# One 256-column product for two layers: node 1's tile times the sending weights of layers 2 and 3 in a four-layer graph kernel

## The chip, the cores and the metric

The kernel runs on one core of one Trainium2 chip. The metric is the device time of one execution in microseconds (us). Three executions of the kernel before took 1271.45, 1272.61 and 1273.16 us, so its median is 1272.61 us.

A core has engines with queues of their own: TensorE (PE in the profile: matmuls, with the loading of their stationary operand listed apart as PEld), VectorE (DVE), ScalarE (ACT), GpSimd (POOL) and SyncE (SP, which here issues DMAs). Matmul results land in PSUM. This kernel treats PSUM as 8 banks, each 128 partitions by 512 fp32 numbers.

## What is computed

x is (32, 512, 128) and adj is (32, 512, 512), symmetric, of zeros and ones. For each of the 32 batches four graph layers follow one another, each as x = x + layer(relu(layernorm(x)), adj): a masked attention, a graph convolution whose weights come out of an LSTM, a block of four "sending and receiving" layers, and a last linear aggregation. The change is in the third, cut here to what matters:

```python
for i in range(4):
    # nodes of layer 0: h; of 1: n1; of 2: [n2, n1]; of 3: [n3, n1, h]
    src_agg = einsum('bjv,bij->biv', nodes @ ws + bs, l2norm(adj, 2))
    dst_agg = einsum('bjv,bji->biv', nodes @ wd + bd, l2norm(adj, 1))
    self_rep = nodes @ wn + bn
    nodes_next = tanh(concat([src_agg, self_rep, dst_agg]) @ wu + bu)
```

With a symmetric adj both aggregations are one. The kernel multiplies the weights together in advance, so that each layer needs one "sending" weight (128x128 per input chunk) and one "own" weight. The inputs by chunk are `CHUNKS = ([0], [1], [2, 1], [3, 1, 0])`: node 1 (the output of layer 0) is an input of layer 2 and again of layer 3.

## The kernel before

The work is cut by batch. A first pass goes over all batches, then an LSTM of 128 steps runs with a second pass over the batches beside it, and the rest, `rest(b, turn, ...)` at L1632, goes through the batches in 32 "turns", one batch each. The chains of several turns overlap.

The order of the instructions is written by a planner (`class Plan`), not by the program text. Each step is handed to it as an op with an engine, a cost in us, what it reads and what it writes (`PE(...)`, `ACT(...)`, `DVE(...)`). The planner takes the ops by rank, which for a turn k grows by 12 per turn and falls with the length of the chain behind the op, and lays them on the engines as they become ready; the result is a fixed order of each engine's queue. It also hands out the buffers. A tile asked for with `bank(...)` takes one of the 8 PSUM banks from the first op that uses it to the end of the last. A rule in `room` keeps the last free bank for ops that are at most 12 in rank behind the most urgent one. `LEAD` is a lift in rank for the last turn's steps that are marked with `R + 4`.

Within a turn, layer i of the third block (L1719 to L1741 in `rest`) has these steps:

- **Fill** (L1012 on ScalarE or L1016 on VectorE, whichever the planner finds earlier): the bias row is copied into a bank `f_py` of 4 x 128 columns, once the layer before has done its L1733.
- **Sending product** (L1726): for each of the four 128-row tiles of the batch, one fp32 matmul with 128 moving columns per input chunk, added on top of the bias. The stationary operand is the node's tile, the moving one the weight. Layers 0 to 3 have 4, 4, 8 and 12 of these. The order of the chunks in layer 3 is nodes 3, 1, 0.
- **Split** (`split`, L1509): ScalarE rounds the bank to fp32r (L1513), and VectorE takes the remainder (L1514), both of 512 columns.
- **Aggregation** (L1555): two times four matmuls of 512 columns, of the rounded part and of the remainder with the squared adjacency `f_ar`, into a bank `f_pa`.
- **Scale** (L1733, VectorE), **own product** (L1737: one fp32 matmul of 512 columns per chunk, into the same bank) and **tanh** (L1741, ScalarE), which makes the next node.

In the trace an fp32 matmul appears as two PE instructions ("passes") with a weight load each, so the 4 products of layer 0 are 8 records, the 12 of layer 3 are 24. An fp32r matmul, such as those of the aggregation, is one record. Some matmul records are missing from the trace. In the names of the profile `f_n` is a node 1, 2 or 3, and `f_T_c` (in a few turns `f_hT_c`) is node 0.

The last turn does its layer 3 in halves of 256 columns (`layer_by_halves`): its splits are L1590 and L1591, its own products are L1609, with 256 moving columns. After the layers a turn transposes node 4 and adds it to x, normalises, aggregates once more (`f_pg`), multiplies (`f_p`, L1791) and stores.

The weights of the sending and own products are in `wf`, 7 chunks by 2 kinds by 128 columns; `W_F = [0, 1, 2, 4]` is the first chunk of each layer, so that node 1's sending weights of layers 2 and 3 are chunks 3 and 5.

Of the kernel before, what the change touches and what calls it, by code (L numbers as in the profile page):

```python
# [13 lines left out]
P = 128  # L14
# [470 lines left out]
FR = mybir.dt.float32r  # L485
# [3 lines left out]
W_F = [0, 1, 2, 4]  # L489
# [304 lines left out]
def symmetric(ctx, tc, x, adj, weights, cols, rows, lstm_b, prelu_a, out, fail):  # L794
# [12 lines left out]
    nc = tc.nc  # L807
    B, N, D = x.shape
    NT = N // P
# [11 lines left out]
    Q_FIRST = range(0)  # L821
    RESIDENT = range(3)
    FIRST_GAPS = (2.0, 3.5, 4.0, 4.0)
    LEAD = 3.0
    Q_AT = 3
    MOVED = range(2, B - 2)
    BY_HALVES = (3,)
    HALVED = 1
    PUT_OFF = (B - 3, B - 2)
    WAITING = (B - 2,)  # L830
    TURN = 32
# [25 lines left out]
    def f32(ap):  # L857
        return ap.bitcast(FP)
# [145 lines left out]
    def fill(rank, dst, src, r, c, after, beside=False):  # L1004

        def mark():
            if not c.marked:
                nc.tensor.matmul(c.t, marks[:, :P], marks[:, : c.size], start=True, stop=True)

        def act():  # L1010
            mark()
            nc.scalar.copy(dst(), src)  # L1012

        def dve():
            mark()
            nc.vector.tensor_copy(dst(), src)  # L1016
        return plan.op({"ACT": (t_act(c.size), act), **({} if beside else {"DVE": (t_dve(c.size), dve)})}, rank, r, [c], after)

    def bias(k, n=NT):
        return brow[:, k, :].unsqueeze(1).to_broadcast([P, n, P])  # L1020
# [155 lines left out]
    def pass_1(b, pos):  # L1176
        R = 10_000 + pos * 10
        xc = new("x", (P, NT, P), f"f_x_{b}")
        n = 2 if pos < HALVED else NT
# [330 lines left out]
    def split(rank, src, name):  # L1510

        parts = new("y", (P, NT, 2, P), f"f_y_{name}", FR)
        ACT(rank, t_act(N), lambda: nc.scalar.copy(parts.t[:, :, 0, :], src.t), [src], [(parts, 0)])  # L1513
        DVE(rank, t_dve(N), lambda: nc.vector.tensor_sub(parts.t[:, :, 1, :], src.t, f32(parts.t[:, :, 0, :])),  # L1514
            [src, (parts, 0)], [(parts, 1)])
        return parts
# [34 lines left out]
    def aggregate(rank, parts, ar, pg):  # L1551

        def half(k):
            for j in range(NT):
                nc.tensor.matmul(pg.t, parts.t[:, j, k, :], ar.t[:, j, :], start=(k == 0 and j == 0),  # L1555
                                 stop=(k == 1 and j == NT - 1))

        def both():
            half(0)
            half(1)  # L1560
        if rank < plan_rest:
            last = PE(rank, 8 * t_r(N), both, [parts, ar], [pg], count=16)
            last.patience = PATIENCE
            return last
        for k in range(2):
            last = PE(rank, 4 * t_r(N), lambda k=k: half(k), [(parts, k), ar], [pg])
        return last

    def state_of(b, lw):
# [5 lines left out]
    def layer_by_halves(R, b, i, nodes, ar, inv_row, before):  # L1575

        nch = L2_CHUNKS[i]
        parts = new("y", (P, NT, 2, P), f"f_y_{b}_{i}", FR)
        for at in range(0, NT, HALF):
            part = slice(at, at + HALF)  # L1580
            py = bank(f"f_py_{b}_{i}_{at}", (P, HALF, P), whole=False, filled=True)
            fill(R, lambda py=py: py.t, bias(i, HALF), [(biases, i)], py, [before])

            def sent(py=py, at=at):
                for j in range(HALF):
                    for c, n in enumerate(CHUNKS[i]):
                        nc.tensor.matmul(py.t[:, j, :], nodes[n].t[:, bass.ts(at + j, P)], wf[:, W_F[i] + c, 0, :], start=False,
                                         stop=(c == nch - 1), skip_group_check=True)
            PE(R, HALF * nch * t_mm(P), sent, [nodes[n] for n in CHUNKS[i]], [py])
            ACT(R, t_act(HALF * P), lambda py=py, part=part: nc.scalar.copy(parts.t[:, part, 0, :], py.t), [py], [(parts, (0, at))])  # L1590
            DVE(R, t_dve(HALF * P), lambda py=py, part=part: nc.vector.tensor_sub(parts.t[:, part, 1, :], py.t, f32(parts.t[:, part, 0, :])),  # L1591
                [py, (parts, (0, at))], [(parts, (1, at))])
        n = new(f"n{i + 1}" if i < 3 else "gs", (P, N), f"f_n{i + 1}_{b}")
        nodes.append(n)
        for at in range(0, NT, HALF):
            cols = slice(at * P, (at + HALF) * P)
            pa = bank(f"f_pa_{b}_{i}_{at}", (P, HALF * P), whole=False)
            for k in range(2):
                for half in range(0, NT, HALF):
                    def quarter(pa=pa, cols=cols, k=k, half=half):  # L1600
                        for j in range(half, half + HALF):
                            nc.tensor.matmul(pa.t, parts.t[:, j, k, :], ar.t[:, j, cols], start=(k == 0 and j == 0),
                                             stop=(k == 1 and j == NT - 1))
                    PE(R, HALF * t_r(HALF * P), quarter, [(parts, (k, half)), ar], [pa], count=2 * HALF)
            before = DVE(R, t_dve(HALF * P), lambda pa=pa, cols=cols: nc.vector.tensor_mul(pa.t, pa.t, inv_row.t[:, cols]), [inv_row], [pa])

            def own(pa=pa, cols=cols):
                for c, m in enumerate(CHUNKS[i]):
                    nc.tensor.matmul(pa.t, wf[:, W_F[i] + c, 1, :], nodes[m].t[:, cols], start=False, stop=(c == nch - 1),  # L1609
                                     skip_group_check=True)  # L1610
# [21 lines left out]
    def rest(b, turn, lw_after):  # L1632
# [81 lines left out]
            n0, before = ln_t(R, xn, "n0", f"c{b}")  # L1714
        nodes = [n0]
        for i, nch in enumerate(L2_CHUNKS):
            if turn == B - 1 and i in BY_HALVES:
                before = layer_by_halves(R + 4, b, i, nodes, ar, inv_row, before)
                continue  # L1719
            py = bank(f"f_py_{b}_{i}", (P, NT, P), filled=True)  # L1720
            fill(R, lambda py=py: py.t, bias(i), [(biases, i)], py, [before])

            def sent(py=py, i=i, nch=nch):
                for j in range(NT):
                    for c, n in enumerate(CHUNKS[i]):
                        nc.tensor.matmul(py.t[:, j, :], nodes[n].t[:, bass.ts(j, P)], wf[:, W_F[i] + c, 0, :], start=False,  # L1726
                                         stop=(c == nch - 1), skip_group_check=True)
            PE(R, 4 * nch * t_mm(P) - 0.01, sent, [nodes[n] for n in CHUNKS[i]], [py])
            parts = split(R, py, f"{b}_{i}")
            pa = bank(f"f_pa_{b}_{i}")  # L1730

            aggregate(R, parts, ar, pa)
            before = DVE(R, t_dve(N), lambda pa=pa: nc.vector.tensor_mul(pa.t, pa.t, inv_row.t), [inv_row], [pa])  # L1733

            def own(pa=pa, i=i, nch=nch):
                for c, n in enumerate(CHUNKS[i]):
                    nc.tensor.matmul(pa.t, wf[:, W_F[i] + c, 1, :], nodes[n].t, start=False, stop=(c == nch - 1),  # L1737
                                     skip_group_check=True)
# [6 lines left out]
        two = turn == B - 1 and 3 in BY_HALVES  # L1745
        if two:
            end4 = update_by_halves(R, b, nodes[4], xc)
        elif moved:
# [194 lines left out]
```

## Time and profile before

| what | value |
|---|---|
| median of three executions | 1272.61 us |
| the profiled execution | 1272.32 us |
| its span, first to last instruction | 1270.4 us |
| PE busy | 1251.3 us, 98% of the span |
| PEld, DVE, ACT, POOL busy | 970.2, 974.8, 835.6, 389.6 us |
| DMA | 232.81 MB, 183 GB/s in the mean |
| granted TensorE clock | 0.999 |
| share of PE in the chain that ended last | 83% |

The page lists groups of instructions as "line engine operation, output<-inputs, shapes, count | busy us, mean ns of one | idle time before them". A mean of one matmul is longer than the distance to the next, since matmuls are pipelined. The distance is read from the chain of waits, which in the last stage runs along PE alone and lists its pieces with start and length.

### The profile page before, as it was taken

What the parts mean: (1) busy time and instruction counts of PE and PEld (TensorE: products, weight loads), DVE (VectorE), ACT (ScalarE), POOL (GpSimd) and SP (SyncE); (2) the same over time, 40 slices, a digit from 0 to 9 for tenths busy, and PEclk for the clock granted to TensorE, in tenths of its full rate; (3) what the DMA queues carried; (4) which work ended last, traced back from release to release, by engine and by line L of the source; (5) the groups of instructions that cost most, each with busy time, mean ns of one, the idle gap of its engine ahead of it and who ended that gap; (6) DMA issues with size and microseconds to landing.
All of it is one profiled execution on the core that took longest, in us unless ns stands there. A gap on an engine that the chain in (4) does not pass through costs nothing.

```text
span 1270.4 us, 33137 instructions
## 1 busy us (share of the span) xinstructions
PE 1251.3 (98%) x12078; PEld 970.2 (76%) x12078; DVE 974.8 (77%) x3267; ACT 835.6 (66%) x2126; POOL 389.6 (31%) x737
## 2 busy tenths in 40 slices
PE   9999999999999999999999999999999999999998
PEld 7988976766776767777778778778787787787776
DVE  7899979889888889775777677677667676787655
ACT  5666777777777766774566666666666666675434
POOL 4565542322322225332213213123123132232101
PEclk9999999999999999999999999999999999999999
DMA  8888887788678778769367677676676677743211
GB/s 291 257 265 275 277 275 225 220 266 254 211 239 283 229 208 211 144 174 219 76 146 176 153 166 164 152 178 152 155 177 154 154 173 158 170 88 96 50 25 45
DMA packets 313725, 232.81 MB, mean 183 GB/s; under 512 B 152145, under 2 KB 258386, under 8 KB 313554
## 3 DMA queue, kind: packets, MB, share of 16 engines
q1 hardware_dynamic: 296096, 213.50, 59.7%
q0 software_dynamic: 16896, 16.78, 8.4%
q8 instruction: 97, 1.59, 0.6%
q14 instruction: 74, 0.61, 0.2%
q10 hardware_dynamic: 562, 0.33, 0.1%
HBM read 136.25 MB, written 62.84 MB: 157 GB/s over the span
## 4 chain that ended last, share of the span: by engine, by line
PE 83%; DVE 7%; DMA 4%; ACT 3%; POOL 2%; issue 1%; SPq 0%; DVEq 0%; ACTq 0%
PE f_pa L1555 17%; PE f_py L1726 15%; PE f_pa L1737 15%; PE f_pg L1555 7%; PE f_s L1421 4%; PE f_po L1427 3%; PE f_z L1315 3%; PE f_pol L1263 2%; PE f_pk L1189 2%; PE f_p L1791 2%; PE f_sl L1253 2%; PE f_pv L1231 2%; PE f_pl L1688 2%; PE f_pd L1288 2%; DMA f_dx<-f_x 1%
## 5 line engine op out<-in xcount | busy, mean ns | idle before, releaser
L1555 PE MATMUL f_pa<-f_ar,f_y 128*128 128x512 f32 x1016 | 295.9, 429 | 0.2 <-DVE f_st_r L1093 0.2
L1555 PEld LDWEIGHTS f_pa<-f_ar,f_y 128*128 128x128 f32 x1016 | 187.9, 188 | 72.9 <-issue 38.3
L1726 PE MATMUL f_py<-f_wf,f_n 128*128 128x128 f32 x1264 | 171.7, 275 | 0.1
L1726 PEld LDWEIGHTS f_py<-f_wf,f_n 128*128 128x128 f32 x1264 | 162.5, 192 | 9.2 <-issue 1.4
L1737 PE MATMUL f_pa<-f_n,f_wf 128*128 128x512 f32 x316 | 150.6, 592 | 0.0
L1741 ACT ACTIVATE f_n<-f_pa,f_bcol 128x512 f32<-128x512 f32 x127 | 88.2, 694 | 92.6 <-PE f_pa L1737 92.6
L1468 ACT ACTIVATE f_ar<-f_a 128x512 fp32r<-128x512 f32 x228 | 141.2, 622 | 6.5 <-DMA f_a<-in_adj_dram 4.3
L1475 POOL DMA_DIRECT2D f_das<-f_ar x32 | 27.1, 845 | 361.2 <-ACT f_ar L1468 356.2
L1513 ACT CAST f_y<-f_py 128x512 fp32r<-128x512 f32 x127 | 74.8, 589 | 80.8 <-PE f_py L1726 78.5
L1514 DVE TENSOR_TENSOR f_y<-f_py,f_y 128x512 fp32r<-128x512 f32 x127 | 87.1, 687 | 48.9 <-ACT f_y L1513 46.2
L1427 PEld LDWEIGHTS f_po<-f_v,f_e 128*32 128x32 f32 x3072 | 91.6, 110 | 27.1 <-issue 20.4
L1427 PE MATMUL f_po<-f_v,f_e 128*32 128x129 f32 x3072 | 109.6, 273 | 1.1 <-DVE f_e L1425 0.7
L1733 DVE TENSOR_TENSOR f_pa<-f_pa,f_inv 128x512 f32<-128x512 f32 x127 | 86.0, 695 | 27.3 <-PE f_pa L1555 27.2
L1421 PE MATMUL f_s<-f_q,f_k 128*32 128x384 f32 x928 | 93.9, 486 | 0.4 <-issue 0.4
L1737 PEld LDWEIGHTS f_pa<-f_n,f_wf 128*128 128x128 f32 x316 | 57.7, 190 | 47.7 <-issue 43.7
L1315 PE MATMUL f_z<-f_w,f_seq 128*32 128x128 f32 x2040 | 83.2, 276 | 7.3 <-DVE f_seq L1361 5.0
L1315 PEld LDWEIGHTS f_z<-f_w,f_seq 128*32 128x32 f32 x2040 | 53.1, 109 | 47.3 <-issue 12.2
L1484 DVE SCALAR_TENSOR_TENSOR f_aT<-f_a,f_aT 128x1024 bf16<-128x1024 f32 (+1 forms) x68 | 76.1, 1153 | 1.2 <-DMA f_aT<-f_das 1.2
L1144 DVE COPY f_hl_d<-f_n 128x1024 uint16<-128x1024 uint16 x28 | 19.4, 694 | 73.7 <-ACT f_n L1741 73.6
L1726 PE MATMUL f_py<-f_wf,f_T_c 128*128 128x128 f32 x448 | 72.8, 275 | 0.1
L1555 PE MATMUL f_pg<-f_ar,f_xp_d 128*128 128x512 f32 x248 | 71.2, 410 | 0.0
L1424 ACT ACTIVATE f_e<-f_s 128x384 f32<-128x384 f32 x128 | 60.7, 484 | 13.1 <-PE f_pg L1555 7.7
(234 smaller groups left out, 2762.1 us busy)
## 6 DMA issues: line engine op xcount, KB each, us to landing
f_a<-in_adj_dram SPq DMA_DIRECT2D x116, 256.0 KB
f_a<-in_adj_dram SPq DMA_DIRECT2D x28, 1024.0 KB
f_das<-f_ar POOLq DMA_DIRECT2D x32, 512.0 KB, 4.7
f_dkq<-f_kh SPq DMA_DIRECT2D x29, 448.0 KB
f_al<-in_adj_dram SPq DMA_DIRECT2D x32, 256.0 KB
f_inv<-f_ddi SPq DMA_DIRECT2D x32, 256.0 KB
f_x<-in_x_dram SPq DMA_DIRECT2D x31, 256.0 KB
out_dram<-f_x SPq DMA_DIRECT2D x31, 256.0 KB
```

The source lines that it names most:

```text
L1315: nc.tensor.matmul(z.t[part, k, :, :], h, w[:, m : m + 4, part], start=False, stop=True, skip_group_check=True)
L1421: PE(R, t_mm(NR), lambda s=s, j=j: quarters(lambda p: nc.tensor.matmul(s.t[p], keys_of()[:, j * P + p.start : j * P + p.stop], q_of(), sta ...
L1427: PE(R, t_mm(P), lambda e=e, t=t, j=j: quarters(lambda p: nc.tensor.matmul(po.t[p, t, :], e.t[:, t * P + p.start : t * P + p.stop], v.t[:, ...
L1468: ACT(rank, 0.62, lambda t=t: nc.scalar.activation(ar.t[:, t, :], a.t[:, t, :], AF.Square, accum_out=deg.t[:, t : t + 1]), [(a, t)], [(ar, ...
L1484: nc.vector.scalar_tensor_tensor(flat(aT.t[:, n * k : n * (k + 1), :]), flat(a.t[:, n * k : n * (k + 1), :]), 1.0, flat(aT.t[:, n * k : n ...
L1513: ACT(rank, t_act(N), lambda: nc.scalar.copy(parts.t[:, :, 0, :], src.t), [src], [(parts, 0)])
L1514: DVE(rank, t_dve(N), lambda: nc.vector.tensor_sub(parts.t[:, :, 1, :], src.t, f32(parts.t[:, :, 0, :])), [src, (parts, 0)], [(parts, 1)])
L1555: nc.tensor.matmul(pg.t, parts.t[:, j, k, :], ar.t[:, j, :], start=(k == 0 and j == 0), stop=(k == 1 and j == NT - 1))
L1726: nc.tensor.matmul(py.t[:, j, :], nodes[n].t[:, bass.ts(j, P)], wf[:, W_F[i] + c, 0, :], start=False, stop=(c == nch - 1), skip_group_chec ...
L1733: before = DVE(R, t_dve(N), lambda pa=pa: nc.vector.tensor_mul(pa.t, pa.t, inv_row.t), [inv_row], [pa])
L1737: nc.tensor.matmul(pa.t, wf[:, W_F[i] + c, 1, :], nodes[n].t, start=False, stop=(c == nch - 1), skip_group_check=True)
L1741: ACT(R, 0.57, lambda pa=pa, n=n, i=i: nc.scalar.activation(n.t, pa.t, AF.Tanh, bias=bcol[:, i : i + 1]), [pa], [n])
```

## The change

In turns 2 to 27, layers 2 and 3 share two banks. Each bank holds two of the four row tiles, and for each tile 128 columns of layer 2 and 128 of layer 3. Both banks are filled with both bias rows before layer 2. In layer 2 each tile of node 1 is multiplied once with 256 columns, the weights of both layers side by side; node 2 follows with 128 columns for layer 2. In layer 3 only nodes 0 and 3 are left, with 128 columns each. The sending products of layer 2 are two PE ops now, one for each bank, and so are those of layer 3. Each layer's split is done bank by bank: two ScalarE copies and two VectorE subtractions of 256 columns instead of one of 512. Aggregation, scale, own product and tanh stay as they are. Besides, `LEAD` goes from 3.0 to 4.0. `HEAD_TILES = 2` and `HALF_TURNS = (B - 1,)` are names for values that were written out before, and `aggregate` now accepts parts with halves of their own.

```diff
-    LEAD = 3.0
+    LEAD = 4.0
...
+    SHARED = range(2, B - 4)
+    HEAD_TILES = 2
+    HALF_TURNS = (B - 1,)
...
-            last = PE(rank, 4 * t_r(N), lambda k=k: half(k), [(parts, k), ar], [pg])
+            last = PE(rank, 4 * t_r(N), lambda k=k: half(k), [(parts, q) for q in parts.parts if (q[0] if isinstance(q, tuple) else q) == k] + [ar], [pg])
...
-            py = bank(f"f_py_{b}_{i}", (P, NT, P), filled=True)
-            fill(R, lambda py=py: py.t, bias(i), [(biases, i)], py, [before])
...
-            PE(R, 4 * nch * t_mm(P) - 0.01, sent, [nodes[n] for n in CHUNKS[i]], [py])
-            parts = split(R, py, f"{b}_{i}")
+            if turn in SHARED and i > 1:
+                if i == 2:
+                    pys = [bank(f"f_py_{b}_2_{h}", (P, 2, 2, P), filled=True) for h in range(2)]
+                    for py in pys:
+                        fill(R, lambda py=py: py.t, brow[:, 2:4, :].unsqueeze(1).to_broadcast([P, 2, 2, P]), [(biases, 2), (biases, 3)], py, [before])
+                for h, py in enumerate(pys):
+                    def sent(py=py, i=i, h=h):
+                        for j in range(2):
+                            of = [bass.ts(2 * h + j, P)] * 3
+                            if i == 2:
+                                nc.tensor.matmul(py.t[:, j, :, :], nodes[1].t[:, of[0]], wf[:, W_F[2] + 1 : W_F[3] + 2 : 2, 0, :], start=False,
+                                                 stop=False, skip_group_check=True)
+                                nc.tensor.matmul(py.t[:, j, 0, :], nodes[2].t[:, of[0]], wf[:, W_F[2], 0, :], start=False, stop=True, skip_group_check=True)
+                            else:
+                                nc.tensor.matmul(py.t[:, j, 1, :], nodes[0].t[:, of[0]], wf[:, W_F[3] + 2, 0, :], start=False, stop=False, skip_group_check=True)
+                                nc.tensor.matmul(py.t[:, j, 1, :], nodes[3].t[:, of[0]], wf[:, W_F[3], 0, :], start=False, stop=True, skip_group_check=True)
+                    PE(R, 2 * (t_mm(2 * P) + t_mm(P)) if i == 2 else 4 * t_mm(P), sent, [nodes[n] for n in ((1, 2) if i == 2 else (0, 3))], [py])
+                parts = new("y", (P, NT, 2, P), f"f_y_{b}_{i}", FR)
+                for h, py in enumerate(pys):
+                    part = slice(2 * h, 2 * h + 2)
+                    ACT(R, t_act(2 * P), lambda py=py, part=part, i=i, parts=parts: nc.scalar.copy(parts.t[:, part, 0, :], py.t[:, :, i - 2, :]), [py], [(parts, (0, h))])
+                    DVE(R, t_dve(2 * P), lambda py=py, part=part, i=i, parts=parts: nc.vector.tensor_sub(
+                        parts.t[:, part, 1, :], py.t[:, :, i - 2, :], f32(parts.t[:, part, 0, :])), [py, (parts, (0, h))], [(parts, (1, h))])
...
```

More of the change, by code (lines that the diff above doesn't have):

```diff
@@ L1178, in pass_1 @@
         xc = new("x", (P, NT, P), f"f_x_{b}")
-        n = 2 if pos < HALVED else NT
+        n = HEAD_TILES if pos < HALVED else NT
         for at in range(0, NT, n):
@@ L1716, in rest @@
         for i, nch in enumerate(L2_CHUNKS):
-            if turn == B - 1 and i in BY_HALVES:
-                before = layer_by_halves(R + 4, b, i, nodes, ar, inv_row, before)
+            if turn in HALF_TURNS and i in BY_HALVES:
+                before = layer_by_halves(R + 4 if turn == B - 1 else R, b, i, nodes, ar, inv_row, before)
                 continue
-            py = bank(f"f_py_{b}_{i}", (P, NT, P), filled=True)
-            fill(R, lambda py=py: py.t, bias(i), [(biases, i)], py, [before])
@@ L1723, in sent @@
[L1723 to L1727, printed above, removed]
-            PE(R, 4 * nch * t_mm(P) - 0.01, sent, [nodes[n] for n in CHUNKS[i]], [py])
-            parts = split(R, py, f"{b}_{i}")
+            if turn in SHARED and i > 1:
[21 more added lines that the diff above has]
+                        parts.t[:, part, 1, :], py.t[:, :, i - 2, :], f32(parts.t[:, part, 0, :])), [py, (parts, (0, h))], [(parts, (1, h))])
+            else:
+                py = bank(f"f_py_{b}_{i}", (P, NT, P), filled=True)
+                fill(R, lambda py=py: py.t, bias(i), [(biases, i)], py, [before])
+                def sent(py=py, i=i, nch=nch):
+                    for j in range(NT):
+                        for c, n in enumerate(CHUNKS[i]):
+                            nc.tensor.matmul(py.t[:, j, :], nodes[n].t[:, bass.ts(j, P)], wf[:, W_F[i] + c, 0, :], start=False,
+                                             stop=(c == nch - 1), skip_group_check=True)
+                PE(R, 4 * nch * t_mm(P) - 0.01, sent, [nodes[n] for n in CHUNKS[i]], [py])
+                parts = split(R, py, f"{b}_{i}")
@@ L1744, in rest @@
             R += 4
-        two = turn == B - 1 and 3 in BY_HALVES
+        two = turn in HALF_TURNS and 3 in BY_HALVES
         if two:
```

## The prediction

> **What bounds the kernel now.** I read the stages first (busy time of each engine in stretches of the span), then PE's waits, then the chain of waits inside one turn.
>
> The stages: start and end, length, then busy us of PE, PEld, DVE, ACT and POOL, the granted clock, the DMA share.
>
> ```profile
> 500.00:540.00 40.00, 39.06 (x283) 31.22 (x282) 32.26 (x98) 27.89 (x66) 17.77 (x24) 1.00 0.73 154
> 540.00:600.00 60.00, 59.89 (x322) 46.08 (x321) 41.42 (x100) 36.04 (x82) 17.04 (x28) 1.00 0.80 194
> 600.00:800.00 200.00, 200.00 (x1083) 156.27 (x1082) 140.15 (x374) 126.88 (x277) 52.70 (x84) 1.00 0.63 148
> 800.00:1000.00 200.00, 200.00 (x1093) 157.16 (x1092) 141.37 (x367) 132.63 (x288) 53.66 (x86) 1.00 0.70 164
> 1000.00:1200.00 200.00, 200.00 (x1075) 156.92 (x1074) 149.00 (x392) 125.97 (x269) 49.61 (x80) 1.00 0.59 127
> ```
>
> From 540 to 1200 us, where turns 2 to 27 run their four layers, PE is busy for 659.89 of 660 us at full clock. DVE has 70 to 75% there, ACT 63 to 66%, POOL about a quarter. The next lines, PE's waits over the whole span that name the sending product, show that it waits once, for 0.4 us, and that is node 0 of a turn outside the change (`f_hT_c`):
>
> ```profile
> PE f_py L1726 <- DVE f_hT_c L915: 0.4, 1, 0.4
> ```
>
> Busy PE is not PE at its peak, so I take the distances from the chain of waits (start, length, what). A turn repeats every 23.28 us (the 24 records of a layer 3 begin at 807.06 and again at 830.34).
>
> ```profile
> 807.06 2.68 PE f_py L1726 x24
> ...
> 811.52 0.89 PE f_py L1726 x8
> ...
> 815.12 1.79 PE f_py L1726 x16
> 816.90 2.77 PE f_pa L1555 x12
> 819.68 3.43 PE f_pa L1737 x8
> ...
> 830.34 2.68 PE f_py L1726 x24
> ```
>
> In the chain the PE pieces touch one another without a gap: 807.06 to 830.34 is all PE work. So in this stage the time is the sum of PE's work, and a turn gets shorter by just what is taken from PE. Whatever shortens ACT, DVE or a turn's own chain gains nothing here.
>
> **The change part by part.**
>
> *The product.* A 128-column pass costs 2.68/24 = 0.1117 us, the same in layer 2 (1.79/16). No row of these turns has an fp32 product of 256 columns, but the last turn has them: its six own products, 12 passes, again from the chain:
>
> ```profile
> 1251.04 2.59 PE f_pa L1609 x12
> ```
>
> That is 2.59/12 = 0.2158 us for a pass of 256 columns; 512 columns cost 3.43/8 = 0.4288. Cost is nearly proportional to columns, and joining saves only a small fixed part. Per turn, node 1's eight products (four of layer 2, four of layer 3) are 16 passes of 0.1117 = 1.787 us. They become four products, 8 passes of 0.2158 = 1.726 us. Saved: 0.061 us a turn, 26 turns: **1.6 us**. The other twelve products keep their 24 passes. Bounds: below, a wide pass at twice a narrow one, 0.2234, saves nothing; above, at half a 512-column pass, 0.2144, 16 x 0.1117 - 8 x 0.2144 = 0.072 us a turn, 1.9 us in all. I take 0.2158, the row with the same width, type and weights.
>
> The Trainium skill, "TensorE: Matmul & The Clock Gate", section "Back-to-back issue gap", says otherwise: in streams with weight loads it gives a sustained 81 ns per matmul of 128 columns and 131 ns per one of 512. A straight line between them puts 256 columns at about 98 ns, an estimate from that page; two passes of 81 would become one of 98, 64 ns less, over 8 x 26 passes 13 us. The rows above, 111.7, 215.8 and 428.8 ns, contradict it for this fp32 work, and the rows decide.
>
> *The moving operand* now comes in two runs of 128 columns, chunks 3 and 5 of `wf`. The LSTM's products read theirs in four runs of 32 columns, and their mean is 276 ns beside 275 ns for a layer's sending product of as many columns in one run:
>
> ```profile
> L1315 PE MATMUL f_z<-f_w,f_seq 128*32 128x128 f32 x2040 | 83.2, 276 | 7.3 <-DVE f_seq L1361 5.0
> L1726 PE MATMUL f_py<-f_wf,f_n 128*128 128x128 f32 x1264 | 171.7, 275 | 0.1
> ```
>
> So broken runs cost at most 1 ns a pass: 8 x 26 x 0.001 = 0.2 us as upper bound, nothing as lower; I take nothing. The Trainium skill speaks against such patterns ("PSUM — Partial Sum Buffer", "Specifications (TRN2)": a non-contiguous access pattern slows matmuls significantly). On the PSUM side the 256 columns are one run here. No row has a 128-wide stationary operand with a broken moving one, so 276 against 275 is the nearest evidence against that rule, not a proof.
>
> *The splits.* The last turn again has the new form, 256 columns (ACT, DVE), beside the old one of 512:
>
> ```profile
> 1245.54 0.37 ACT L1590 CAST f_y<-f_py 128x256 fp32r<-128x256 f32 x1 [0.65 <-PE f_py L1587]
> ```
> ```profile
> 1245.94 0.42 DVE L1591 TENSOR_TENSOR f_y<-f_py,f_y 128x256 fp32r<-128x256 f32 x1 [1.86 <-ACT f_y L1590]
> ```
> ```profile
> L1513 ACT CAST f_y<-f_py 128x512 fp32r<-128x512 f32 x127 | 74.8, 589 | 80.8 <-PE f_py L1726 78.5
> L1514 DVE TENSOR_TENSOR f_y<-f_py,f_y 128x512 fp32r<-128x512 f32 x127 | 87.1, 687 | 48.9 <-ACT f_y L1513 46.2
> ```
>
> A turn gets 2 x (0.74 - 0.589) = 0.30 us more on ACT and 2 x (0.84 - 0.687) = 0.31 us more on DVE. Both have 5.8 us or more free in a turn of 23.28 us, since they are at most 75% busy, and PE's order always holds another turn's work. I cost it at nothing. Without that cover, the most would be the 0.30 + 0.31 us standing before PE in each turn: 26 x 0.61 = 16 us. The first half of a layer can be split while the second is multiplied, which shortens the turn's own chain; PE is full, so that gains nothing either.
>
> *The fills* are the same two copies a turn, of 512 columns each, only that layer 3's comes earlier. *Layer 2 grows and layer 3 shrinks* by four tiles' products, moved about 15 us ahead within the same turn: no change of PE's sum. *More ops* mean more waits at PE's queue: each of the four sending ops waits for its bank. Behind them on PE stands the work of all turns. Where the planner's costs hold, they are met early, as they are now (0.4 us for the whole span). No DMA is added, and none is moved past a queue by the text; the planner may shift their places.
>
> *The order.* `LEAD` touches only the last turn's marked steps. There PE's chain is also closed, up to the last matmul at 1264.2 us, and 7 of its records after 1258 us are warming matmuls (0.67 + 0.88 us). Bounds: the lift may save at most that 1.6 us, and may cost one step's wait, 0.9 us (one `f_p` product of 8 records); I take nothing.
>
> *Sum*, against the profiled execution: 1272.3 - 1.6 = 1270.7 us. The median of the three runs lies 0.3 us above that execution, so I forecast **1271.0 us**.
>
> **The rivals.**
>
> *A. The banks run short (slower).* The two banks are held from before layer 2 until layer 3 is split. In this trace, for one turn:
>
> ```profile
> 807.90 0.68 DVE L1016 COPY f_py<-f_brow 128x512 f32<-128x512 f32 x1
> ...
> 817.56 0.69 DVE L1514 TENSOR_TENSOR f_y<-f_py,f_y 128x512 fp32r<-128x512 f32 x1
> ...
> 825.50 1.11 ACT L1012 COPY f_py<-f_brow 128x512 f32<-128x512 f32 x2
> ...
> 833.73 0.69 DVE L1514 TENSOR_TENSOR f_y<-f_py,f_y 128x512 fp32r<-128x512 f32 x1 [1.01 <-ACT f_y L1513]
> ```
>
> Layer 2's bank is taken from 807.90 to 818.25 (10.4 us), layer 3's from 825.50 to 834.42 (8.9 us). After: two banks from 807.90 to 834.42, 2 x 26.5 = 53 bank-us in place of 19.3. Divided by 23.28 us that is 1.45 banks more, in the mean. From the same listing I added up the other bank uses of a turn (layers 0 and 1 about 20, the four `f_pa` about 39, `f_pg`, `f_p` and `f_pl` about 15 bank-us): with the 19.3 it is 93 bank-us or 4.0 of 8 banks now, 5.5 after, with stretches at all 8 (an estimate, from laying these intervals over one another). For this rival: those peaks, and the rule on the last free bank, which holds back the very ops of later turns that keep PE full. Against it: the fills may come later than they do now (this one stands 7 us before its product), and PE has three turns' work to choose from. If a bank comes free late by one half split (0.42 us) in each turn, the loss is 26 x 0.42 = 10.9 us, and the time 1272.6 + 10.9 - 1.6 = 1281.9. It decides from 1.6/26 = 0.06 us a turn, and counts as slower (by over 0.2%, 2.5 us, about what a measurement of this kernel can tell from no change) from 4.1/26 = 0.16 us a turn, 1275.1 us.
>
> *B. More is gained than the passes.* The new order may also close PE gaps: 0.94 us in 500 to 540, up to 1.6 us in warming matmuls. Then 1271.0 - 0.9 = 1270.1 to 1268.5 us; middle 1269.3. Against it: almost all the stage has no gap to close.
>
> *C. The change gives nothing*: the wide pass costs twice the narrow one, or 1.6 us is lost in shifted order: 1272.6 us.
>
> **How the numbers follow.** Forecast (1270.2 to 1272.0): 0.43. C (1272.0 to 1275.1): 0.17. B: 0.18. A: 0.22. Faster by over 0.2% (under 1270.1) is B: 0.18; same is forecast and C: 0.60; slower is A: 0.22. The range takes in B, the forecast, C and the lower edge of A, leaving out the dear end of A and a little of B: 1268.8 to 1276.0.
>
> **What would show it.** The wide product's records at a distance of 0.216 us (0.223 or more speaks for C). A turn period of 23.22 us in place of 23.28. PE busy for 200 of 200 us in the three long stretches; with A there is idle PE time before `f_pa` or `f_py` that ends with a fill or an L1514-like subtraction, on the new lines. The splits at 0.37 and 0.42 us with no PE wait ended by them. The prediction is wrong if PE has waits of over 2 us in sum between 540 and 1200 us, or if the sum of PE's work outside `f_py` changes.

## The result, and the profile after

The changed kernel is slower, by about a third of one per cent. The median of its 21 executions is 1276.9 us (1272.46 to 1283.85), the ratio to the kernel before is 1.0032 with a 95% interval of 1.0024 to 1.0041. The forecast was 1271.0 us, with a range up to 1276.0. The profiled execution took 1280.9 us with a span of 1279.0 us. It lies at the slow end of the kernel's own executions, so its whole distance to the profile before, 8.6 us of span, is more than the 4.3 us by which the medians differ.

I read the same views as before, first the stages (start and end, length, busy us of PE, PEld, DVE, ACT and POOL, granted clock, DMA share, GB/s):

```profile
540.00:600.00 60.00, 55.58 (x271) 42.37 (x270) 38.85 (x99) 32.62 (x78) 19.63 (x31) 0.94 0.80 174
600.00:800.00 200.00, 200.00 (x1020) 154.34 (x1019) 151.65 (x398) 118.87 (x282) 50.48 (x82) 1.00 0.64 152
800.00:1000.00 200.00, 200.00 (x1009) 154.06 (x1008) 153.03 (x400) 117.67 (x280) 50.73 (x82) 1.00 0.72 160
1000.00:1200.00 200.00, 200.00 (x1035) 155.97 (x1034) 154.55 (x409) 123.93 (x288) 54.64 (x84) 1.00 0.58 135
```

From 600 to 1200 us all is as forecast: PE is never idle and the clock is full. The loss is in the stretch before it, where PE lacks 4.4 us and the clock falls to 0.94 in the mean. Nearly all of PE's missing time there is one wait of an aggregation:

```profile
PE f_pa L1558 <- DVE f_y L1744: 4.4, 1, 4.4
```

PE's timeline around it, with the idle time in brackets, and VectorE's beside it:

```profile
585.63 2.42 PE L1558 MATMUL f_pa<-f_ar,f_y 128*128 128x512 f32 x8
592.48 2.07 PE L1558 MATMUL f_pa<-f_ar,f_y 128*128 128x512 f32 x4 [4.42 <-DVE f_y L1744]
```
```profile
584.20 0.68 DVE L1019 COPY f_py<-f_brow 128x512 f32<-128x512 f32 x1
591.38 0.74 DVE L1147 COPY f_T_c<-f_hT_c 128x1024 uint16<-128x1024 uint16 x1 [6.50 <-DMA f_hT_c<-f_hl_c]
592.01 0.74 DVE L1744 TENSOR_TENSOR f_y<-f_py,f_y 128x256 fp32r<-128x256 f32 x2
```

PE waits for the two halved remainders of turn 2's layer 3. Their inputs are there since 585.7 us, when ScalarE ended its second cast, but VectorE's queue is a fixed order, and ahead of them stands a copy that makes node 0 of turn 5, three turns away. That copy stands for 6.5 us, because the transposing DMA that it reads (`f_hT_c<-f_hl_c`) has not landed. SyncE's timeline shows why. These are DMA issues, first of the kernel after, then of the kernel before:

```profile
577.44 0.64 SPq L1650 DMA_DIRECT2D f_x<-f_dl  x1
578.13 0.48 SPq L1830 DMA_DIRECT2D out_dram<-f_x  x1
581.79 0.32 SPq L1649 DMA_DIRECT2D f_x<-f_dx  x1
582.15 0.43 SPq L1650 DMA_DIRECT2D f_x<-f_dl  x1
582.70 1.23 SPq L1152 DMA_TRANSPOSE f_hT_c<-f_hl_c  x1
```
```profile
576.17 1.27 SPq L1149 DMA_TRANSPOSE f_hT_c<-f_hl_c  x1
577.48 0.58 SPq L1803 DMA_DIRECT2D out_dram<-f_x  x1
580.67 0.32 SPq L1646 DMA_DIRECT2D f_x<-f_dx  x1
```

Before, the transfer is issued first. After, an output store of turn 1 and two loads of `f_x` are issued ahead of it. The loads go into the buffer that the store reads, so they wait for its landing; SyncE's waits in the stretch 540 to 600 us have the line

```profile
SPq L1649 <- DMA out_dram<-f_x: 6.0, 2, 3.1
```

and the transfer stands behind the waiting loads, though its own source was ready at about 579.7 us. Issued at 582.70, it is used only at 591.38, 8.7 us later. Before, it was used 3.8 us after its issue at 576.17, and VectorE's copy waited 1.86 us for it:

```profile
580.01 0.76 DVE L1144 COPY f_T_c<-f_hT_c 128x1024 uint16<-128x1024 uint16 x1 [1.86 <-DMA f_hT_c<-f_hl_c]
```

The planner takes 3.0 us as the time of this transfer and nothing for the landing of a store (`gap=3.0`, `gap=0.0`), so it reckoned neither with the 3.1 us of the loads' wait nor with the 8.7 us.

So the transfer is late twice: it is issued later, and it takes longer. It is the longer landing that PE feels. An estimate from these rows: had it landed 3.8 us after its issue, as before, the copy could have begun at 586.5 us; PE's aggregation began 1.1 us after the copy (592.48 after 591.38), that is at 587.6 us, and PE had work until 588.06. The later issue by itself would then have cost PE nothing. How the long landing came about is taken up at the end of the section on the prediction.

The loss has a second part besides the wait. The same stages, cut finer:

```profile
588.00:592.50 4.50, 0.08 (x2) 0.02 (x1) 1.12 (x3) 0.04 (x1) 0.00 (x0) 0.92 1.14 150
592.50:595.00 2.50, 2.50 (x6) 2.02 (x7) 1.37 (x4) 0.55 (x1) 0.00 (x0) 0.50 0.04 6
595.00:600.00 5.00, 5.00 (x18) 3.94 (x18) 3.33 (x7) 0.74 (x2) 0.00 (x0) 0.64 0.91 197
600.00:605.00 5.00, 5.00 (x21) 3.22 (x20) 1.23 (x3) 1.66 (x3) 0.00 (x0) 1.00 0.58 191
```

After the idle time PE works at half clock: all of 592.5 to 595, and by the mean of 0.64 about 3.6 us of the next 5. Half of the 6.1 us or so is lost, 3.1 us more. PE counts as busy there, so the busy column alone doesn't show it. In the second profile of the changed kernel (again, below) the clock falls earlier in the idle time, and only 4.5 us of work run at half clock, 2.2 us lost.

The pair of profiles (8.6 us of span) then reads: 4.4 idle, 3.1 half clock, 1.05 in the tail from the start of the last matmul (6.51 before, 7.56 after), 2.7 that the profile after is already late at an earlier transfer of the same kind (issued at 549.1 us before, 551.8 after). Back come 26 x 0.09 = 2.3 from shorter turns, and 0.7 at the end of PE's chain, where lead (below) has the last matmul 0.7 us earlier. The sum is 8.3, where 8.6 were measured. The 2.7 us are not the change's: up to about 565 us the orders of PE, ACT, DVE, POOL and SP are the same in both kernels, and this transfer comes at 549 to 553 us over all profiles of this study, at 549.8 in the second profile of the changed kernel. To leave such differences out, I count below from the issue of that transfer ("the transfer at 549 us") to the start of the last matmul.

### The profile page after: what moved, and what is told of

Its sections match the earlier page's. It is cut to its first block, busy times and chain, and to the rows that moved or that the text cites. A ratio compares the mean times of both kernels' runs of the same rounds, so it can differ in the third digit from the quotient of the medians.

```text
span 1279.0 us, 32755 instructions
## 1 busy us (share of the span) xinstructions
PE 1251.9 (98%) x11870; PEld 966.0 (76%) x11870; DVE 1005.4 (79%) x3352; ACT 810.1 (63%) x2145; POOL 390.0 (30%) x737
## 4 chain that ended last, share of the span: by engine, by line
PE 86%; DVE 6%; DMA 2%; ACT 2%; POOL 2%; issue 1%; SPq 0%; DVEq 0%; ACTq 0%
PE f_pa L1558 18%; PE f_pa L1764 15%; PE f_pg L1558 8%; PE f_py L1753 6%; PE f_s L1424 4%; PE f_po L1430 4%; PE f_z L1318 4%; PE f_py L1733 4%; PE f_pol L1266 2%; PE f_p L1818 2%; PE f_pk L1192 2%; PE f_sl L1256 2%; PE f_pv L1234 2%; PE f_py L1735 2%; PE f_pl L1691 2%; PE f_py L1738 2%
## 5 line engine op out<-in xcount | busy, mean ns | idle before, releaser
L1743 ACT CAST f_y<-f_py 128x256 fp32r<-128x256 f32 x104 | 38.2, 367 | 76.2 <-PE f_py L1735 61.1
L1558 PE MATMUL f_pg<-f_ar,f_xp_d 128*128 128x512 f32 x248 | 74.2, 437 | 0.0
L1517 DVE TENSOR_TENSOR f_y<-f_py,f_y 128x512 fp32r<-128x512 f32 x75 | 51.2, 685 | 22.8 <-ACT f_y L1516 22.7
L1558 PE MATMUL f_pg<-f_ar,f_xp_c 128*128 128x512 f32 x256 | 68.5, 407 | 0.1
L1733 PE MATMUL f_py<-f_wf,f_n 128*128 128x256 f32 x208 | 63.6, 388 | 0.0
L1119 ACT ACTIVATE f_xn_c<-f_x,f_sh_c,f_rs_c 128x128 f32<-128x128 f32 x131 | 57.1, 486 | 8.6 <-DVE f_sh_c L1127 8.2
L1558 PEld LDWEIGHTS f_pg<-f_ar,f_xp_d 128*128 128x128 f32 x248 | 46.4, 188 | 21.0 <-issue 8.6
```

Source lines behind the costliest of these rows:

```text
L1733: nc.tensor.matmul(py.t[:, j, :, :], nodes[1].t[:, of[0]], wf[:, W_F[2] + 1 : W_F[3] + 2 : 2, 0, :], start=False, stop=False, skip_group_c ...
```

## The experiments

Each ratio is to the kernel before, run on the same chip beside it. The median of the kernel before was 1274.0, 1273.71 and 1274.48 us in the three sets. My theory was the queue: the new order of SyncE's issues makes the transfer late, VectorE's queue hands the delay to PE, the clock adds to it, and the product itself gains what was forecast. The rivals: the halved work or the two held banks cost in every turn; `LEAD` costs at the end; the profile's wait was a chance of one execution.

### First set: the wait, the order, `LEAD`

**again** is the changed kernel as it is.

> The changed kernel once more, for a second profile. Theory W (a late transfer): the changed order issues one transposing transfer of node 0 (turn 5) behind an output store and a load that waits for it; VectorE's copy waits for the landing, a split of layer 3 stands behind that copy, PE waits 4.4 us for the split and its clock is then halved for some 7 us. If so, the same PE wait of 2 to 5 us stands at 585 to 590 us in this profile too, the turn period in the long stretch is again 23.19 us (23.28 before), and the time is 1275 to 1278 us. Rival S (the sharing itself costs, by banks or by the halved splits): PE waits or a longer period in many turns between 600 and 1200 us. Rival E (chance): the wait is absent and the time is as before, 1272 to 1273 us. The 2.5 us by which the first profile was late at 500 us, with the same order up to there, should be absent if they were chance.

1278.65 us, ratio 1.0036 [1.0021, 1.0052]; the time is a little above what I expected. The wait is there again, with the same length:

```profile
PE f_pa L1558 <- DVE f_y L1744: 4.5, 1, 4.5
```

So it belongs to the order and not to one execution.

**swap** is the changed kernel with the two loads issued just behind the transfer instead of ahead of it. All else of the order stays.

```diff
         order.sort(key=lambda o: (o.start, o.no))
+        def issue(name, k=0):
+            return [o for o in order if o.engine == "SP" and any(c.name == name for c in o.cells)][k]
+        loads = [issue("f_x3_5", 0), issue("f_x3_5", 1)]
+        order[:] = [o for o in order if o not in loads]
+        at = order.index(issue("f_hT_c1")) + 1
+        order[at:at] = loads
```

> The changed kernel with two instructions of one queue exchanged in place: the two loads of x for a later turn are issued behind turn 5's transfer of node 0 and no longer ahead of it. Nothing else moves. Theory W: the transfer starts about 3 us earlier and lands before VectorE needs it, PE's wait at 588 us and the halved clock are gone: 4.4 + 3.4 us less than the first profile, 1269.5 to 1271.5 us, that is 1.5 to 2.5 us faster than the kernel before. Rival S or L (LEAD): the time stays at 1275 to 1278 us.

1272.93 us, 0.9985 [0.9968, 1.0002]. Two issues moved in one queue take away the whole loss, 5.7 us against the changed kernel of the same set (1278.65). Against the kernel before only 1.1 us are left, less than I expected, and the interval reaches to no difference. The wait of `f_T_c` and the half clock are gone; PE waits 0.7 and 0.4 us, both at other places. Halving and banks are unchanged in this kernel, so they can't be the loss.

**late_before** is the opposite: the kernel before, with the transfer put behind the store and the two loads.

```diff
         order.sort(key=lambda o: (o.start, o.no))
...
+        late = [issue("f_hT_c1"), issue("f_x3_5", 0), issue("f_x3_5", 1)]
+        at = order.index(late[1])
+        order[at + 1 : at + 1] = [late[2], late[0]]
+        del order[max(i for i, o in enumerate(order) if o is late[2])]
+        order.remove(late[0])
```

> The kernel before, without the change, but with the changed kernel's place for that one transfer: the store, then the two loads that wait for it, then turn 5's transfer of node 0. Theory W: the loss appears without the change, a DVE wait on the transfer of several us, a PE wait behind it, and 1274 to 1280 us. Rivals S and L: 1272 to 1273 us, no wait.

1276.17 us, 1.0018 [1.0003, 1.0033]. VectorE's wait comes with the order, without any wide product, halved split or shared bank; a line of VectorE's waits and one of PE's, from 540 to 1200 us:

```profile
DVE f_T_c L1151 <- DMA f_hT_c<-f_hl_c: 7.5, 1, 7.5
```
```profile
PE f_pa L1744 <- DVE f_pa L1740: 1.4, 1, 1.4
```

But only 1.4 us of the 7.5 reach PE, and the clock stays full. The late transfer costs about 2 us in the old order and 6 in the new. Two things differ, and no run separates them. One is what PE finds to do meanwhile: in the new order the next aggregation in PE's queue needs the two remainders behind the copy, in the old one PE has other work up to a scale (L1740). The other is the landing: the transfer is issued at 583.47 us here and used at 587.78, with the copy waiting for it, so it took 4.3 us, not 8.7:

```profile
583.47 1.23 SPq L1156 DMA_TRANSPOSE f_hT_c<-f_hl_c  x1
```
```profile
587.78 0.76 DVE L1151 COPY f_T_c<-f_hT_c 128x1024 uint16<-128x1024 uint16 x1 [7.50 <-DMA f_hT_c<-f_hl_c]
```

So late_before shows that the queue place alone makes VectorE wait and costs about 2 us; the full loss it doesn't reproduce.

**lead** is the kernel before with one line of the change.

```diff
-    LEAD = 3.0
+    LEAD = 4.0
```

> The kernel before with LEAD = 4.0 alone. Theory W and the prediction: within 0.6 us of the kernel before, 1272 to 1273 us. Rival L (the lift of the last turn's steps makes the loss): 1275 us or more, with PE idle after 1200 us.

1274.24 us, 0.9999 [0.9984, 1.0014]: nothing, and no wait of PE from 520 us on. In its profile the last matmul comes 0.7 us earlier after the transfer at 549 us (714.04 us, before 714.78), and the tail behind it is longer (6.99 us, before 6.51); the last product there is 16 records in one piece, before it was 8.

### Second set: the parts of the wait, and the product by itself

**copy_last** is the changed kernel with the waiting copy moved behind the two remainders in VectorE's queue; the transfer stays late.

```diff
         order.sort(key=lambda o: (o.start, o.no))
+        copy = [o for o in order if o.engine == "DVE" and any(c.name == "f_T_c1" for c in o.cells)][0]
+        order.remove(copy)
+        subs = [i for i, o in enumerate(order) if o.engine == "DVE" and any(c.name == "f_y_25_3" for c in o.cells)]
+        order.insert(subs[1] + 1, copy)
```

> The changed kernel with one VectorE instruction moved: the copy that waits for turn 5's late transfer stands behind the two splits of turn 2's layer 3 and no longer ahead of them. The transfer stays late (8.7 us from issue to copy). Theory W, in its form that the harm is the place in VectorE's queue: PE no longer waits for the splits; next in line is the scaling of the same layer, behind the copy, with some 4.5 us of PE work in between, so a wait of at most 1 us remains, the clock is not halved, and the time is 1.0 to 2.5 us under the kernel before. If the lateness of the transfer itself counted (turn 5 needs node 0), a wait of 3 to 4 us would stand at its layer 0 instead.

1273.92 us, 1.0009 [0.9997, 1.0021]. The copy still waits, and PE waits for a scale behind it:

```profile
DVE f_T_c L1151 <- DMA f_hT_c<-f_hl_c: 4.5, 1, 4.5
```
```profile
PE f_pa L1768 <- DVE f_pa L1764: 1.2, 1, 1.2
```

The 4.4 us and the half clock are gone, so the queue place of the remainders is what carried the wait to PE. The gain against the kernel before that I expected did not come: 1.2 + 0.5 us of PE waits are left, which would still leave some 1 us of gain. In the profile that is there (713.87 us from the transfer at 549 us to the last matmul, before 714.78); in the times it is not, with a tail of 7.45 us behind it, 0.9 more than before.

**warm** is the changed kernel with 22 small matmuls in PE's queue between the two parts of the aggregation that waits, which keep PE at work during the wait. They add zeros to the bank, so what is computed stays the same.

```diff
-    def aggregate(rank, parts, ar, pg):
+    def aggregate(rank, parts, ar, pg, zeros=0):
...
+            for _ in range(zeros if k else 0):
+                nc.tensor.matmul(pg.t, marks[:, :P], marks, start=False, stop=False, skip_group_check=True)
...
-            aggregate(R, parts, ar, pa)
+            aggregate(R, parts, ar, pa, 22 if turn == 2 and i == 3 else 0)
```

> The changed kernel with 22 matmuls of zeros, bf16, 512 columns, 0.216 us each (4.75 us), added on top of the bank ahead of the aggregation that waits, so that PE is busy while it waits. They add nothing to the sum; the order of all other instructions is the same. It splits theory W's loss in two: the wait itself (4.4 us) stays, the halved clock (6.8 us at half speed, 3.4 us) should go. Expected: 3 us faster than the changed kernel, 1.0 to 2.0 us slower than the kernel before, clock 1.00 in the profile at 590 to 600 us. If the clock does not matter, it is as slow as the changed kernel, 4.5 us over the kernel before.

1275.98 us, 1.0024 [1.0014, 1.0034]. VectorE still waits 5.9 us for the transfer, so the wait itself is there; but the clock is full in the same stretches:

```profile
588.00:592.50 4.50, 4.50 (x23) 2.96 (x22) 3.03 (x7) 0.59 (x1) 0.00 (x0) 1.00 0.40 88
592.50:595.00 2.50, 2.50 (x14) 1.92 (x13) 2.50 (x6) 0.75 (x2) 0.00 (x0) 1.00 0.99 195
595.00:600.00 5.00, 5.00 (x21) 3.21 (x21) 1.43 (x3) 1.66 (x3) 0.00 (x0) 1.00 0.95 271
```

From the transfer at 549 us to the last matmul it takes 716.6 us, in again 718.7: 2.1 us less, although the filled time is 4.8 us, 0.3 longer than again's idle time. The loss by the clock is 2 to 3 us; the medians of the two sets, 1278.65 and 1275.98, differ by 2.7, over different runs. Against the kernel before, 2.3 us are left by the medians, a little more than the 1.0 to 2.0 I expected.

**swap_narrow** is swap with node 1's product of layer 2 and of layer 3 as two products of 128 columns, in the same place of the same order.

```diff
+                                for q in range(2):
+                                    nc.tensor.matmul(py.t[:, j, q, :], nodes[1].t[:, of[0]], wf[:, W_F[2 + q] + 1, 0, :], start=False,
+                                                     stop=False, skip_group_check=True)
-                                nc.tensor.matmul(py.t[:, j, :, :], nodes[1].t[:, of[0]], wf[:, W_F[2] + 1 : W_F[3] + 2 : 2, 0, :], start=False,
-                                                 stop=False, skip_group_check=True)
```

> The kernel swap (loads behind the transfer) with each 256-column product written as two of 128 columns again, into the same banks, with the same splits, fills and order of everything else. It prices the wide product alone. The prediction's 0.061 us a turn gives a period of 23.25 us and 1.6 us more than swap; the 0.087 us by which the turn got shorter in the trace gives 23.28 us and 2.3 us more. If the gain came from the order or the splits, the period stays 23.19 us and the time that of swap.

1273.53 us, 0.9999 [0.9991, 1.0008]; **swap2**, which is swap once more beside it:

> The kernel swap again, beside the others on one chip and for a second profile. Theory W: no PE wait over 1 us after 540 us, turn period 23.19 us, and 1.5 to 2.5 us faster than the kernel before (the first five rounds gave about 2 us, with an interval that reached to no difference).

1272.93 us, 0.9998 [0.9988, 1.0008]. The gain of 1.5 to 2.5 us on the kernel before that I expected doesn't show (0.8 by the medians), and the times do not part swap2 and swap_narrow. The chains of waits do (start, length, what). First swap_narrow, then swap2, for one tile of layer 2 of the same turn:

```profile
818.18 0.44 PE f_py L1740 x4
818.63 0.22 PE f_py L1742 x2
818.85 0.45 PE f_py L1740 x4
```
```profile
817.53 0.43 PE f_py L1739 x2
817.96 0.22 PE f_py L1741 x2
818.18 0.43 PE f_py L1739 x2
```

Four narrow passes take 0.445 us, two wide ones 0.43. From the starts of successive products a turn has 23.25 us in swap_narrow and 23.19 in swap2: 0.060 us a turn for the wide product. Before it is 23.28; the other 0.03 us go with the order: in swap2 and swap_narrow the last aggregation of a turn stands in one piece, before it was two. First swap2's chain, then that of the kernel before:

```profile
803.15 1.83 PE f_pg L1564 x8
```
```profile
824.92 0.93 PE f_pg L1555 x4
...
828.50 0.93 PE f_pg L1555 x4
```

That is 1.83 against 2 x 0.93, the 0.03 us. The swap also shows the queue without the delay. In swap2's SyncE timeline the transfer goes out 3.0 us earlier than the changed kernel's, and VectorE's timeline has the copy without a wait:

```profile
578.12 0.50 SPq L1836 DMA_DIRECT2D out_dram<-f_x  x1
579.70 1.24 SPq L1158 DMA_TRANSPOSE f_hT_c<-f_hl_c  x1
581.32 0.33 SPq L1655 DMA_DIRECT2D f_x<-f_dx  x1
```
```profile
584.67 0.74 DVE L1153 COPY f_T_c<-f_hT_c 128x1024 uint16<-128x1024 uint16 x1
585.30 0.78 DVE L1750 TENSOR_TENSOR f_y<-f_py,f_y 128x256 fp32r<-128x256 f32 x2
```

### Third set: the planner told the landing times

**told** is the changed kernel with truer landing times for the first turns; the planner then finds the order itself.

```diff
-    def by_transfer(rank, src, c, tag, name):
+    def by_transfer(rank, src, c, tag, name, gap=3.0):
...
-                [apart], [turned], gap=3.0)
+                [apart], [turned], gap=gap)
...
-            n0, before = by_transfer(R, lambda: flat(xn.t), xn, "n0", f"c{b}")
+            n0, before = by_transfer(R, lambda: flat(xn.t), xn, "n0", f"c{b}", 5.0 if turn < 6 else 3.0)
...
-                return ACT(R, 0.5, store, mine, [], gap=0.0) if at else DMA(R, 64 * n, store, mine, [], gap=0.0)
+                return ACT(R, 0.5, store, mine, [], gap=0.0) if at else DMA(R, 64 * n, store, mine, [], gap=4.0 if turn < 2 else 0.0)
```

> The changed kernel, with the planner told what the traces show of landings: node 0's transfers of turns 2 to 5 land 5.0 us after their issue instead of 3.0, the output stores of turns 0 and 1 take 4.0 us instead of none. The planner lays the order anew from there. Theory W: turn 5's transfer is issued ahead of the second store, no DVE wait on it over 2 us, no PE wait over 1 us after 540 us, period 23.19 us: 1 to 2.5 us faster than the kernel before. If new orders in general lose what the product gains, it is 1274 us or more.

1271.57 us, 0.9975 [0.9964, 0.9987]: this version is faster than the kernel before, and by the ratios (1.0032 and 1.0036) than the changed kernel too. By the medians it gains 2.9 us, a little more than I expected. PE has no idle time from 540 to 1200 us; the stages, of which the first is shown, have PE busy for 60.00 and three times 200.00 us:

```profile
540.00:600.00 60.00, 60.00 (x307) 45.73 (x306) 41.72 (x104) 36.71 (x85) 17.86 (x29) 1.00 0.82 190
```

**gap9** tells the planner only of the one transfer, as `by_transfer(..., 9.0 if turn == 5 else 3.0)`, and nothing of the store.

> The changed kernel, with the planner told only that turn 5's transfer of node 0 lands 9.0 us after its issue. Its copy is laid later in VectorE's queue and the transfer is issued earlier. Theory W: no wait on it, 0.5 to 2.5 us faster than the kernel before. If the wait moves to another transfer, the profile names it, and the time is 1 us or more over the kernel before.

1273.34 us, 0.9985 [0.9971, 0.9999]. The transfer is now issued at 569.7 us, ahead of the store, and its copy comes 11.4 us later without a wait; PE waits 0.2 us. One number in the planner's costs, for one transfer, undoes the loss too.

**told_lead3** is told with `LEAD = 3.0`.

> As told, with LEAD = 3.0 again. In the runs with LEAD = 4.0 the last matmul came 0.7 us earlier and the end after it took 0.5 us longer. Expected: within 0.6 us of told, the stretch after the last matmul 6.5 to 6.9 us.

1271.88 us, 0.9976 [0.9962, 0.9989], the same as told, and the tail is 6.7 us, as expected.

**told_before** is the kernel before with the landing times of told.

> The kernel before, told the same landings as told: a control. Theory W: no wait was there to remove, so 1272 to 1274 us, within 0.6 us of the kernel before, and told is 1.0 to 2.0 us faster than this one. If told_before is as fast as told, the gain lies in the order and not in the wide product.

1274.41 us, 1.0004 [0.9990, 1.0018]: without the change the truer times bring nothing, since there was no such wait to take away. So told against told_before is the worth of the change without its wait: 2.8 us by the medians, or 2.5 with told_lead3, which has the same `LEAD` as told_before. From the transfer at 549 us to the last matmul it is 712.74 us in told, 713.31 in told_lead3 and 715.27 in told_before. With equal `LEAD` that is 2.0 us, where 26 turns of 0.09 us are 2.3. Of these 0.09 us the wide product is 0.06 and the order 0.03.

## Why the prediction was wrong

- **The product: right.** Forecast 0.061 us a turn from 16 passes of 0.1117 and 8 of 0.2158; swap_narrow against swap2 gives 0.060, and two wide passes take 0.43 us in the chain.
- **The moving operand in two runs at nothing: right.** A wide pass at 0.215 us is no longer than the 0.2158 of the last turn's products, whose operand is in one run. The rule against broken patterns that the prediction cites stands among the properties of PSUM; on that side the wide product writes one run, so these runs say nothing about it.
- **The step that failed** is the sentence "No DMA is added, and none is moved past a queue by the text; the planner may shift their places", after which I costed the shift at nothing, together with "where the planner's costs hold, they are met early". The planner did shift them. A transfer fell behind a store's landing in SyncE's queue and then took 8.7 us to land, its copy held VectorE's queue, PE waited 4.4 us, and its clock was halved. What I put at nothing cost 5.7 us (again against swap), more than the change gains. The profile before held the warning: in its SyncE timeline a load waits 2.6 us for the landing of a store (issued at 577.48, the load at 580.67 us) directly behind this very transfer, and the copy already waits 1.86 us for the transfer there. I looked at PE's waits only, which show how far a queue's delay reached PE in the old order and say nothing of a new one.
- **The splits at nothing: right with a condition.** ACT and DVE have the room I gave them (in the first stage, 540 to 600 us, a little more: the row has DVE at 69% and ACT at 60%, where I wrote 70 to 75 and 63 to 66), and PE waits for no split in the long stages. The cover that I named, "PE's order always holds another turn's work", was gone just where VectorE's queue was held by something else; I priced its loss for all turns (16 us) and not for one place.
- **The clock: not in the sum.** I gave no price to a wait above its length. An idle time of 4.4 us cost 4.4 and some 2 to 3 us more (3.1 and 2.2 by the two profiles of the changed kernel).
- **Rival A, the banks: right sign, wrong mechanism.** No wait of PE on a fill or a bank appears, and swap, with the same banks held, loses nothing. Its time of 1281.9 us was far off.
- **Rival B: in part.** The new order gives 0.03 us a turn of its own (0.8 us in all), not from idle PE but, by the chains, from the aggregation in one piece. The changed kernel has it too (23.19 us a turn), under its loss.
- **Rival C, nothing gained:** refuted for the product. swap and swap2 are the same kernel; with 0.9985 [0.9968, 1.0002] and 0.9998 [0.9988, 1.0008] the measurement alone does not tell its gain from none, told's does.
- **`LEAD` at nothing: right**, in lead and, against told, in told_lead3.
- **What would show it** held its own test: "PE waits of over 2 us in sum between 540 and 1200 us" was named as the sign of a wrong forecast, and it is what came.

What stays open is why the transfer took 8.7 us to land. One thing goes with it: where GpSimd's transfer of `f_das` (512 KB) stands. In seven profiles the copy waited for the transfer, so that the time from issue to copy is its landing:

| run | `f_das` issued, against the transfer | from issue to copy |
|---|---|---|
| before, lead | 1.4 and 1.6 us after it | 3.8 and 3.9 us |
| late_before | 3.75 us ahead of it | 4.3 us |
| copy_last, warm | 0.2 and 0.3 us ahead | 8.3 us both |
| after, again | 0.5 and 0.6 us ahead | 8.7 us both |

The rows for after, before and late_before:

```profile
582.21 0.83 POOL L1478 DMA_DIRECT2D f_das<-f_ar  x1 [2.33 <-ACT f_ar L1471]
```
```profile
577.59 0.83 POOL L1475 DMA_DIRECT2D f_das<-f_ar  x1 [1.61 <-ACT f_ar L1468]
```
```profile
579.72 0.83 POOL L1482 DMA_DIRECT2D f_das<-f_ar  x1 [1.61 <-ACT f_ar L1475]
```

So the new order put the transfer just behind `f_das`, and swap put it 2.4 us ahead again. But no run moved `f_das` alone, so that it is the cause is argued only. Nor is it settled how the longer tail from the last matmul on (6.5 to 6.8 us with `LEAD` at 3, 7.0 to 8.0 at 4) and the last matmul's earlier place share the zero of `LEAD`; no run times the two apart.

## What to carry to other kernels

When a planner writes the order, a change of a few instructions is a change of the order. So compare the order of the DMA issues too: look for a load that waits for a store's landing, what stands behind it in that queue, which engine's queue holds the consumer, and which large transfer of another queue now goes out just ahead of it. Give the planner landing times from the trace, not issue costs. And price a wait of PE beyond its length: one of several microseconds may bring a stretch at half clock after it.

## What the runs showed of the hardware

- **The clock.** In both profiles of the changed kernel an idle time of PE (4.4 and 4.5 us) was followed by half clock, for 6.8 us in all. In the first it began 3.7 us into the idle time and lasted 6.1 us into the work, in again it began 2.1 us into the idle time (which starts at 586.09 us) and lasted 4.5 us into the work. The stretches at its two ends, first of the first profile, then of again:

```profile
591.50:592.00 0.50, 0.00 (x0) 0.00 (x0) 0.50 (x1) 0.00 (x0) 0.00 (x0) 0.79 1.28 290
598.50:599.00 0.50, 0.50 (x4) 0.38 (x4) 0.00 (x0) 0.00 (x0) 0.00 (x0) 0.88 0.79 172
```
```profile
588.00:588.50 0.50, 0.00 (x0) 0.00 (x0) 0.00 (x0) 0.00 (x0) 0.00 (x0) 0.73 0.33 4
595.00:595.50 0.50, 0.50 (x5) 0.45 (x4) 0.50 (x1) 0.20 (x1) 0.00 (x0) 0.95 1.26 287
```

An idle time of 1.4 us, in late_before, left the clock at 1.00, and so did the filled wait in warm. The Trainium skill, "TensorE: Matmul & The Clock Gate", section "What's actually happening", has the clock halved after an idle window of about 3.4 us and freed after a busy one of about the same length. The runs agree with that in part: 4.4 us of idle time halved the clock and 1.4 us did not. But in again it fell after 2.1 us of idle time, less than such a window, and the work at half clock lasted 4.5 and 6.1 us, more than one. So an idle time need not reach 3.4 us to bring half clock; the threshold itself these runs do not show.
- **A transposing transfer has no fixed time.** The same 128x1024 transfer landed 3.8 us after its issue before, 4.3 in late_before and 8.3 to 8.7 in copy_last, warm and the two profiles of the changed kernel.
- **Aggregations in one piece are cheaper.** Eight fp32r matmuls of 512 columns in a row take 1.83 us, in two groups of four with other work between 2 x 0.93 us.
